# A rotation block whose end is factored into 64-wide products, with doubled squarings on TensorE and identity products written to unread PSUM

## The chip, the cores and the metric

The kernel runs on one core of a Trainium2 chip. The metric is device time in microseconds (us) of that core for one execution; of several executions the median is given. A profile is one further execution, recorded by the hardware profiler.

## The reference

Four layers run one after the other on `x` (4 batches, 512 rows, 288 channels), steered by `cond` (4, 288), all in float32. The change touches the first layer and the start of the second:

```python
U, _ = jnp.linalg.qr(P)                        # P: (288, 64)
v = silu(cond) @ W.T + b                       # 2016 numbers for each batch
A[:, iu, ju], A[:, ju, iu] = v, -v             # skew, (4, 64, 64)
R = expm(A)
z = jnp.einsum('btn,nd->btd', x, U)
z_rot = jnp.einsum('btd,bde->bte', z, R)
x = x + jnp.einsum('btd,nd->btn', z_rot - z, U)
```

Layers two to four are transformer blocks: layer norm with a shift and a scale made from `cond`, attention with 16 heads of width 18, and a feed-forward part of 1152; in the last block each row goes to two of four experts.

## The kernel before

**Layout.** `x` stays in SBUF as four tiles x0 to x3 (128 partitions, NT = 4 groups of rows, C = 288 channels). PSUM has three pools: `pmm` (one bank, 3 buffers), `pbig` (two banks, 2 buffers) and `pacc` (one bank, 1 buffer). In the rotation block and in what follows it, `pinned` is set, and every instruction of TensorE, VectorE and ScalarE goes through the helper at L60 that keeps it in the order in which it is written; so nearly all rows of the profile carry L60, and are told apart by the names of their tiles.

**The QR (L561 on).** It works on the 64x64 Gram matrix of P, one column i at a time, with two broadcasts on TensorE. `gram_step(i+1)` sends row i+1 of X to all 64 partitions (`to_all`, tile g_bc, a product of one column of the identity and the row), and VectorE makes rn, a column of Fm and the new X from it; ScalarE makes a column of Nm, GpSimd one of Rh. Then row i of Wt is broadcast in the same way (w_bc), and `sign_step` makes Hs, den, num, rec, c and the new Wt on VectorE. X, Wt and Fm of a column are needed by the next, so the columns form a chain.

**Beside the columns** run three generators, each taken a step further at fixed places of a column. `main` is `skew_and_exp`: it transposes W (p_WT), makes v (p_v), goes through DRAM to the skew matrices (p_up, then tile S, once column 33 has been reached), and then the exponential: nine products of a series (p_ser) and SQUARINGS = 16 squarings (p_sq). Since E stands for expm minus the identity, a squaring is E2 = 2E + E·E; `products` does the eight 64x64 products of the four batches on TensorE, two batches side by side in the array, and VectorE adds 2E while it evicts. `side` is `project_P` (the transposes p_t of x, and p_zP, the product of P and x) and later `first_modulations` (p_mod). `fills` clears buffers.

**The rotation's end (L582 to L598).** The 64x64 half of X that holds the elimination is transposed (p_E), copied (Em), multiplied with At, which is P transposed (p_Q), and scaled into QT (64x288). Es holds expm minus the identity of all batches with the signs Hs applied, XD the right half of X.

**`rotate(n)` (L601 to L626)** takes batches 2n and 2n+1. Each has a product Es·QT (p_RU, 64x288), a copy to RU on ScalarE, and a product with XD (p_EU); then for each of the four groups of rows one product p_xr with zP for each batch and a VectorE add into x, for both batches in turn.

**The start of attention (L1264 on).** `rotate(0)` is run to its end; then `head_biases(0)` (products p_qkb), the statistics of batch 0 (`normalize(0, 0, 0)`), and `project(0)`: transposes p_t, products p_qk and p_v, and a trip of q and k through DRAM (tiles qd). `rotate(1)` and the statistics of batch 1 are interleaved with the products of `project(0)` once q and k have been sent. Then LOOK = 10 steps of `maxima` follow (a pair of products p_s, 128x1024, and a VectorE reduce of each), each with one step of what is left of `rotate(1)`. After that the main loop over the 12 pairs of block and batch begins.

The helper behind both broadcasts of a column:

```python
def to_all(name, i, src):
    p = pbig(name)[:D, 0, :src.shape[-1]]
    matmul(p, ident[:D, i:i + 1].to_broadcast([D, D]), src, start=True, stop=True)
    return p
```

Of the kernel before, what the change touches and what calls it, by code (L numbers as in the profile page):

```python
# [9 lines left out]
F32 = mybir.dt.float32  # L10
U32 = mybir.dt.uint32
AF = mybir.ActivationFunctionType
ALU = mybir.AluOpType
# [3 lines left out]
B, T, C = 4, 512, 288  # L17
NT = 4
KC, KP = 3, 96

KW, TAIL, STRIPS = 2, 32, 3
# [12 lines left out]
D = 64  # L34
# [13 lines left out]
def cond_seq_kernel(ctx: ExitStack, tc: tile.TileContext, a: dict, out: bass.AP):  # L48
    nc = tc.nc
# [14 lines left out]
    vector, scalar = InOrder(nc.vector), InOrder(nc.scalar)  # L64
    matmul, transpose = InOrder(nc.tensor).matmul, InOrder(nc.tensor).transpose
# [7 lines left out]
    work = ctx.enter_context(tc.tile_pool(name="work", bufs=2))  # L73
    mods = ctx.enter_context(tc.tile_pool(name="mods", bufs=1))
    ps = ctx.enter_context(tc.tile_pool(name="ps", bufs=2, space=PSUM))
    blocks = ctx.enter_context(ExitStack())
    fixed = blocks.enter_context(tc.tile_pool(name="fixed", bufs=1))

    def pmm(name):
        return ps.tile([128, 512], F32, tag="mm", name=name, bufs=3)  # L80

    def pbig(name):
        return ps.tile([128, 2, 512], F32, tag="big", name=name)

    def pacc(name):
        return ps.tile([128, 512], F32, tag="acc", name=name, bufs=1)
# [11 lines left out]
    x = []  # L98
# [5 lines left out]

    ident = const.tile([128, 128], F32, name="ident")
    make_identity(nc, ident)
    ones = const.tile([1, 128], F32, name="ones")
    nc.gpsimd.memset(ones, 1.0)
    eps6 = const.tile([128, 1], F32, name="eps6")
# [92 lines left out]
    def head_biases(l):  # L202
        QB[l] = to_columns(f"qkb{l}", WA[l][3])
        if l != 1:
            vector.tensor_mul(QB[l], QB[l], scol)
# [155 lines left out]
    with tc.tile_pool(name="l0", bufs=1) as l0, tc.tile_pool(name="l0w", bufs=2) as l0w, \  # L361
            tc.tile_pool(name="scratch", bufs=1, space=bass.MemoryType.DRAM) as scratch:

        X = l0.tile([D, 2 * D], F32, name="X")
        At = l0.tile([D, C], F32, name="At")
        Wt = l0.tile([D, D], F32, name="Wt")
        pt = pmm("p_G")
        for k in range(KC):  # L370
# [5 lines left out]
            transpose(pt[:D, k * KP:(k + 1) * KP], P_in[:, k, :], ident[:KP, :KP])  # L376
        nc.vector.tensor_copy(Wt, pt[:D, :D])
        nc.scalar.copy(At, pt[:D, :C])
        minus = l0.tile([D, D], F32, name="minus")
        nc.gpsimd.memset(minus, -1.0)  # L380
        nc.gpsimd.affine_select(out=minus, in_=minus, compare_op=ALU.is_gt, fill=0.0, base=0,
# [4 lines left out]
        Hs = l0.tile([D, D], F32, name="Hs")  # L386

        def to_all(name, i, src):
            p = pbig(name)[:D, 0, :src.shape[-1]]
            matmul(p, ident[:D, i:i + 1].to_broadcast([D, D]), src, start=True, stop=True)  # L390
            return p

        def gram_step(i):
            bc = to_all(f"g_bc{i}", i, X[:, i:i + D + 1])
            rn = l0w.tile([D, 1], F32, tag="rn", name=f"rn{i}")
            vector.reciprocal(rn, bc[:, 0:1])
            vector.scalar_tensor_tensor(Fm[:, i:i + 1], X[:, i:i + 1], rn, minus[:, i:i + 1], ALU.mult, ALU.mult)
            vector.scalar_tensor_tensor(X[:, i + 1:i + D + 1], bc[:, 1:], Fm[:, i:i + 1],
                                        X[:, i + 1:i + D + 1], ALU.mult, ALU.add)
            scalar.activation(Nm[:, i:i + 1], bc[:, 0:1], AF.Sqrt, scale=0.25)  # L400
            nc.gpsimd.tensor_mul(Rh[:, i:i + 1], Fm[:, i:i + 1], Nm[:, i:i + 1])
# [15 lines left out]
        def skew_and_exp():  # L417
# [48 lines left out]
            nc.gpsimd.affine_select(out=up, in_=up, compare_op=ALU.is_gt, fill=0.0, base=0,  # L466
                                    pattern=[[0, B], [1, D]], channel_multiplier=-1)
            yield
            while column[0] < 33:
                yield  # L470
                yield
            pt = pmm("p_up")
# [11 lines left out]
            vector.tensor_scalar_mul(Sf[:, :2 * D], Sf[:, :2 * D], 0.5 ** SQUARINGS)  # L484
            yield

            def products(name, left, right):
                p = pacc(name)
                for m in range(4):
                    for h in range(2):  # L490
                        r = slice(h * D, (h + 1) * D)
                        matmul(p[r, m * D:(m + 1) * D], left[r, (m + 2) % 4, :], right[r, m, :],
                                         start=True, stop=True)
                return p[:, :4 * D]


# [5 lines left out]
                vector.scalar_tensor_tensor(E.rearrange("i m j -> i (m j)"), p, 1.0 / n, Sf, ALU.mult, ALU.add)  # L502
                yield
            for n in range(SQUARINGS):
                p = products(f"p_sq{n}", E, E)
                E2 = l0w.tile([128, 4, D], F32, tag="E", name=f"sq{n}")
                yield
                vector.scalar_tensor_tensor(E2.rearrange("i m j -> i (m j)"), E.rearrange("i m j -> i (m j)"),
                                            2.0, p, ALU.mult, ALU.add)
                yield  # L510
                E = E2

# [1 line left out]
            for b in range(B):  # L514
                scalar.copy(Eb[:, b, :], E[(b % 2) * D:(b % 2 + 1) * D, 2 + b // 2, :])
            Rm.append(Eb)


        zP = hT[1][:, 0:2, :]
        XD, Es = hT[1][0:D, KW, 0:D], hT[1][0:D, KW, D:5 * D].rearrange("p (b d) -> p b d", b=B)  # L520
        rnorm = hT[1][0:D, KW, 5 * D:5 * D + 1]
        QT = mods.tile([D, C], F32, name="QT")

        def project_P():
            for n in range(2):
# [35 lines left out]
        for i in range(D):  # L561
            column[0] = i
            if i + 1 < D:
                gram_step(i + 1)
            bc = to_all(f"w_bc{i}", i, Wt[:, i:])
            beside = i >= 6 and (i < 15 or i >= 18)
            next(main, None)
            if beside:
                next(side, None)
            sign_step(i, bc)  # L570
            next(main, None)
            if beside:
                next(side, None)
            next(fills, None)
            if i == 27:

                WA.append(load_attn(0, "L1_cond_W_qkv", "L1_cond_b_qkv", "L1_cond_W_proj", "L1_cond_b_proj"))
        for _ in main:
            pass
        for _ in side:  # L580
            pass
        preload()  # L582

        dg = l0.tile([D, 2], F32, name="dg")
        norm, sign4 = dg[:, 0:1], dg[:, 1:2]
        junk = l0.tile([D, D], F32, name="junk")
        pt = pmm("p_E")
        transpose(pt[:D, :D], X[:, D:], ident[:D, :D])
        Em = l0.tile([D, D], F32, name="Em")
        scalar.copy(Em, pt[:D, :D])  # L590
        vector.scalar_tensor_tensor(junk, Nm, 2.0, ident[:D, :D], ALU.mult, ALU.mult, accum_out=norm)
        vector.reciprocal(rnorm, norm)
        vector.scalar_tensor_tensor(junk, Hs, 4.0, ident[:D, :D], ALU.mult, ALU.mult, accum_out=sign4)
        vector.scalar_tensor_tensor(Es, Rm[0], sign4,
                                    Hs.rearrange("p (o d) -> p o d", o=1).to_broadcast([D, B, D]), ALU.mult, ALU.mult)
        pt = pmm("p_Q")
        matmul(pt[:D, :C], Em, At, start=True, stop=True)
        vector.tensor_scalar_mul(QT, pt[:D, :C], rnorm)  # L598
        scalar.copy(XD, X[:, D:])


    def rotate(n):

        ts = []
        for h in range(2):
            p = pmm(f"p_RU{2 * n + h}")
            matmul(p[:D, :C], Es[:, 2 * n + h, :], QT, start=True, stop=True)
            t = work.tile([128, C], F32, tag="gated", name=f"RU{2 * n + h}", bufs=3)
            scalar.mul(t[:D], p[:D, :C], rnorm)
            ts.append(t)  # L610
        yield 0.6
        e = work.tile([128, C], F32, tag="gate", name=f"EU{n}")
        p = pmm(f"p_EU{n}")
        for h in range(2):
            matmul(p[h * D:(h + 1) * D, :C], XD, ts[h][:D], start=True, stop=True)
        scalar.copy(e, p[:, :C])
        yield 0.6
        for j in range(NT):
            ps = pmm(f"p_xr{2 * n}_{j}"), pacc(f"p_xr{2 * n + 1}_{j}")
            for h in range(2):  # L620
                r = slice(h * D, (h + 1) * D)
                matmul(ps[h][:, :C], zP[r, n, j * 128:(j + 1) * 128], e[r], start=True, stop=True)
            for h in range(2):
                xb = x[2 * n + h][:, j, :]
                vector.tensor_add(xb, ps[h][:, :C], xb)
            yield 0.6  # L626

# [377 lines left out]
    with tc.tile_pool(name="attn", bufs=2) as at:  # L1007
# [90 lines left out]
        def maxima(G, step):  # L1098

            n, g = divmod(G, NG)  # L1100
            j, hp = divmod(step, 2)
            p = pbig(f"p_s{G}_{step}")
            for i in range(2):
                r = slice((2 * hp + i) * HS, (2 * hp + i + 1) * HS)
                matmul(p[:, i, :], Q[n % 2][r, g, j * 128:(j + 1) * 128], K[n % 2][r, g, :], start=True, stop=True)
            vector.tensor_reduce(M[G % 2][:, j, 2 * hp:2 * hp + 2, HD:HD + 1], p, AX.X, ALU.max)
# [155 lines left out]
            yield from route(b)  # L1262

        E, ready, PO, S, there, norms = [], [], [None], {}, set(), {}  # L1264
        for _ in rotate(0):
            pass
        head_biases(0)
        norm = normalize(0, 0, 0)
        for _ in norm:
            pass  # L1270
        norm1 = normalize(0, 0, 1)
        rest = rotate(1)
        sent = False
        for cost in project(0, norm):
            next(norm1, None)
            sent = sent or cost is None
            if sent and cost == 0.95:
                next(rest, None)
        norm = norm1
        for t in range(LOOK):  # L1280
            maxima(*divmod(t, 8))
            if t == 8:
                take_maxima(0)
            next(norm, None)
            next(rest, None)
# [212 lines left out]
```

## Time and profile before

| | value |
|---|---|
| three executions, us | 2103.7, 2110.49, 2111.6 |
| their median, us | 2110.49 |
| the profiled execution, us | 2122.64 |
| its span, first to last recorded work, us | 2120.9 |
| mean granted TensorE clock over the span | 0.933 |
| PE (TensorE products) busy, us | 1933.4 (91%) |
| PEld (weight loads, beside PE) busy, us | 936.0 (44%) |
| DVE (VectorE) busy, us | 933.8 (44%) |
| ACT (ScalarE) busy, us | 777.1 (37%) |
| POOL (GpSimd) busy, us | 251.3 (12%) |

The profiler's page gives these as busy time over the whole span. It also cuts the span into 40 equal slices of 53 us and writes for each engine one digit, its busy share in tenths, and in the row PEclk the granted clock in tenths of full speed. The most time by far goes to the attention and the feed-forward parts; the largest group of instructions is this one (the line of the source, engine and operation, output and inputs, shape, count, busy us and mean ns of one, then the idle time ahead of it on its engine and what ended that):

```profile
L60 DVE TENSOR_REDUCE store<-p_s 128x2 f32<-128x1024 f32 x384 | 470.2, 1225 | 385.1 <-PE p_st L60 334.0
```

The rotation block and the start of attention fill about the first 226 us. The timeline view lists single instructions there: start (us), duration (us), engine, line, operation, and output and inputs with their shapes; an entry with "x2" stands for a product or a weight load that is recorded as two.

### The profile page before, as it was taken

What the parts mean: (1) busy time and instruction counts of PE and PEld (TensorE: products, weight loads), DVE (VectorE), ACT (ScalarE), POOL (GpSimd) and SP (SyncE); (2) the same over time, 40 slices, a digit from 0 to 9 for tenths busy, and PEclk for the clock granted to TensorE, in tenths of its full rate; (3) what the DMA queues carried; (4) which work ended last, traced back from release to release, by engine and by line L of the source; (5) the groups of instructions that cost most, each with busy time, mean ns of one, the idle gap of its engine ahead of it and who ended that gap; (6) DMA issues with size and microseconds to landing.
All of it is one profiled execution on the core that took longest, in us unless ns stands there. A gap on an engine that the chain in (4) does not pass through costs nothing. (4 is left out here: it accounts for less than half of the span.)

```text
span 2120.9 us, 26102 instructions
## 1 busy us (share of the span) xinstructions
PE 1933.4 (91%) x10200; PEld 936.0 (44%) x10200; DVE 933.8 (44%) x1974; ACT 777.1 (37%) x1159; POOL 251.3 (12%) x361
## 2 busy tenths in 40 slices
PE   7778989999999999899999999998987899999997
PEld 4553322343433434334234343333322367777775
DVE  6774535526256263552643626355577134111111
ACT  5111444434345354443543434434444222112111
POOL 1000001000001020110100000000010122332322
PEclk9556899999999999989999999999999689999999
DMA  3211125122031121511213112161221355666563
GB/s 95 70 39 45 34 65 160 26 56 76 16 75 41 52 79 45 127 46 25 88 27 77 48 51 81 21 135 31 81 51 58 111 196 178 203 207 223 182 216 94
DMA packets 89418, 187.21 MB, mean 88 GB/s; under 512 B 25453, under 2 KB 50456, under 8 KB 86802
## 3 DMA queue, kind: packets, MB, share of 16 engines
q1 hardware_dynamic: 77462, 103.39, 18.8%
q0 software_dynamic: 11248, 79.79, 11.6%
q10 hardware_dynamic: 584, 2.36, 0.4%
q8 instruction: 80, 1.31, 0.3%
q14 instruction: 44, 0.36, 0.1%
HBM read 152.49 MB, written 55.45 MB: 98 GB/s over the span
## 5 line engine op out<-in xcount | busy, mean ns | idle before, releaser
L60 ACT ACTIVATE e<-p_st 128x1024 f32<-128x1024 f32 x384 | 392.7, 1023 | 692.1 <-PE p_st L60 687.8
L60 DVE TENSOR_REDUCE store<-p_s 128x2 f32<-128x1024 f32 x384 | 470.2, 1225 | 385.1 <-PE p_st L60 334.0
L60 PE MATMUL p_s<-store 32*128 32x512 f32 x1536 | 452.6, 664 | 79.7 <-DVE store L60 76.9
L60 PE MATMUL p_st<-store 32*128 32x512 f32 x1536 | 449.8, 664 | 0.9 <-DVE store L60 0.9
L60 PEld LDWEIGHTS p_s<-store 32*128 32x128 f32 x1536 | 122.7, 190 | 312.5 <-DVE store L60 221.4
L60 PE MATMUL p_av<-e,store 128*32 128x512 f32 x1536 | 213.5, 629 | 2.2 <-ACT e L60 2.2
L60 PE MATMUL p_he<-hTe,store 128*128 128x256 f32 (+1 forms) x1026 | 200.1, 404 | 4.2 <-DVE hTe L60 4.2
L60 PE MATMUL p_ye<-store,hide 128*128 128x288 f32 x684 | 175.0, 415 | 7.1 <-ACT hide L60 7.1
L60 ACT ACTIVATE hide<-p_he,store 128x256 f32<-128x256 f32 x171 | 68.5, 471 | 281.8 <-PE p_he L60 281.8
L60 PEld LDWEIGHTS p_he<-hTe,store 128*128 128x128 f32 (+1 forms) x1026 | 147.6, 191 | 53.1 <-issue 30.5
L691 POOL TENSOR_TENSOR x<-x,gated 128x288 f32<-128x288 f32 x80 | 63.4, 793 | 848.0 <-DVE gated L60 848.0
L60 PE MATMUL p_qk<-hT,wqk 128*126 128x512 f32 (+1 forms) x360 | 163.9, 626 | 0.0
L60 PE MATMUL p_h<-hT,w 128*128 128x512 f32 (+1 forms) x432 | 156.7, 618 | 5.2 <-DVE store L60 5.2
L60 PEld LDWEIGHTS p_ye<-store,hide 128*128 128x128 f32 x684 | 130.3, 193 | 46.9 <-ACT hide L60 10.9
L60 PE MATMUL p_y<-w,hid 128*128 128x288 f32 x576 | 141.8, 407 | 0.0
L60 DVE TENSOR_TENSOR gated<-p_y,gate 128x288 f32<-128x288 f32 x32 | 14.6, 457 | 285.8 <-PE p_y L60 285.8
L60 PEld LDWEIGHTS p_st<-store 32*128 32x128 f32 x1536 | 119.5, 189 | 12.4 <-issue 9.3
L60 PEld LDWEIGHTS p_y<-w,hid 128*128 128x128 f32 x576 | 108.8, 190 | 35.5 <-issue 6.1
L60 PEld LDWEIGHTS p_h<-hT,w 128*128 128x128 f32 (+1 forms) x432 | 60.7, 189 | 99.7 <-issue 83.6
L60 PE MATMUL p_o<-wp,oc 126*128 126x288 f32 (+1 forms) x288 | 101.2, 475 | 1.3 <-DVE oc L60 1.3
L60 PEld LDWEIGHTS p_qk<-hT,wqk 128*126 128x126 f32 (+1 forms) x360 | 47.8, 179 | 98.7 <-issue 98.5
L60 DVE COPY hTe<-p_te 128x512 f32<-128x512 f32 x19 | 13.1, 690 | 172.9 <-PE p_tf L60 127.8
(248 smaller groups left out, 1736.6 us busy)
## 6 DMA issues: line engine op xcount, KB each, us to landing
store<-qd SPq DMA_DIRECT2D x96, 144.0 KB
qd<-stage SPq DMA_DIRECT2D x48, 252.0 KB
od<-o SPq DMA_DIRECT2D x192, 36.0 KB
rd<-rd SPq DMA_DIRECT2D x12, 576.0 KB
oc<-od SPq DMA_DIRECT2D x24, 252.0 KB
rb<-rd SPq DMA_DIRECT2D x24, 252.0 KB
etab<-in_L_cond_w_dram SPq DMA_DIRECT2D x4, 1296.0 KB
etab<-in_L_cond_w_dram SPq DMA_DIRECT2D x8, 576.0 KB
```

The costliest lines, as they stand in the source:

```text
L60: ins = f(*args, **kw)
L691: nc.gpsimd.tensor_add(x[b][:, j, :], x[b][:, j, :], t)
```

## The change

- A new helper `keep_warm(bank, n)` issues products of the 128x128 identity with itself, n columns in all, at most 512 in one product, into a bank that nobody reads.
- One of them, of 256 columns (384 in columns 0 to 2, 29 to 32 and 52 to 63), is put into every column of the QR, after `sign_step`; its target is the second bank of the w_bc tile, which `to_all` hands out through `free`.
- `products` takes `twice`: 2E is added on TensorE, by a product of twice the identity (`two`) and E into the same PSUM tile, for both halves of the array; a squaring is then evicted by a ScalarE copy in place of VectorE's operation.
- The series may start at column 30 instead of 33, and `head_biases(0)` moves from behind `rotate(0)` into column 60.
- The rotation's end is factored in another way: Y is the right half of X with norms and signs applied, p_RY = R_b·Y and p_MT are 64x64 products for each batch, and MT·At gives what p_EU gave. p_E, p_Q, Em, QT, Es, p_RU and RU go. The diagonal of Nm is reduced in the last column.
- `rotate` does all of its first batch before its second, with two groups of rows in one `pbig` tile; of batch 0 each group is added on its own, of the others two at a time. Batch 0's statistics are interleaved with its adds.
- `keep_warm` is also put in at six places between the rotation's end and the last step of `maxima`.

```diff
+    def keep_warm(bank, n):
+
+        while n > 0:
+            w = min(n, 512)
+            matmul(bank[:, :w].rearrange("p (o m) -> p o m", m=128), ident, ident_wide[:, :w // 128, :], start=True, stop=True)
+            n -= w
...
+        two = l0.tile([128, 128], F32, name="two")
+        nc.gpsimd.tensor_scalar_mul(two, ident, 2.0)
...
         def to_all(name, i, src):
-            p = pbig(name)[:D, 0, :src.shape[-1]]
+            t = pbig(name)
+            p = t[:D, 0, :src.shape[-1]]
             matmul(p, ident[:D, i:i + 1].to_broadcast([D, D]), src, start=True, stop=True)
+            free[0] = t[:, 1]
             return p
...
-            while column[0] < 33:
+            while column[0] < 30:
...
-            def products(name, left, right):
+            def products(name, left, right, twice=False):
+
                 p = pacc(name)
+                halves = [slice(h * D, (h + 1) * D) for h in range(2)]
+                if twice:
+                    for r in halves:
+                        matmul(p[r, :4 * D], two[r, r], right[r].rearrange("i m j -> i (m j)"), start=True, stop=False)
                 for m in range(4):
-                    for h in range(2):
-                        r = slice(h * D, (h + 1) * D)
+                    for r in halves:
                         matmul(p[r, m * D:(m + 1) * D], left[r, (m + 2) % 4, :], right[r, m, :],
-                                         start=True, stop=True)
+                               start=not twice, stop=not twice or m == 3)
...
-                p = products(f"p_sq{n}", E, E)
+                p = products(f"p_sq{n}", E, E, twice=True)
...
-                vector.scalar_tensor_tensor(E2.rearrange("i m j -> i (m j)"), E.rearrange("i m j -> i (m j)"),
-                                            2.0, p, ALU.mult, ALU.add)
+                scalar.copy(E2.rearrange("i m j -> i (m j)"), p)
...
             bc = to_all(f"w_bc{i}", i, Wt[:, i:])
             beside = i >= 6 and (i < 15 or i >= 18)
+            warm = free[0]
...
+            keep_warm(warm, 384 if i < 3 or i >= 52 or 29 <= i < 33 else 256)
             next(fills, None)
...
+            if i == D - 4:
+                head_biases(0)
...
+        vector.scalar_tensor_tensor(junk, Hs, 2.0, ident[:D, :D], ALU.mult, ALU.mult, accum_out=dg[:, 2:3])
+        Y = l0.tile([D, D], F32, name="Y")
+        vector.tensor_scalar(Y, X[:, D:], dg[:, 1:2], dg[:, 2:3], ALU.mult, ALU.mult)
+        pt = pmm("p_RY")
+        for b in range(B):
+            matmul(pt[:D, b * D:(b + 1) * D], Rm[0][:, b, :], Y, start=True, stop=True)
+        warm = pbig("warm1")
+        keep_warm(warm[:, 0], 256)
+        RY = l0.tile([D, B * D], F32, name="RY")
+        vector.tensor_copy(RY, pt[:D, :B * D])
+        pt = pmm("p_MT")
+        for b in range(B):
+            matmul(pt[:D, b * D:(b + 1) * D], RY[:, b * D:(b + 1) * D], Y, start=True, stop=True)
+        keep_warm(warm[:, 0], 256)
+        vector.tensor_copy(MT, pt[:D, :B * D])
...
+            m = slice((2 * n + h) * D, (2 * n + h + 1) * D)
+            matmul(p[h * D:(h + 1) * D, :C], MT[:, m], At, start=True, stop=True)
         scalar.copy(e, p[:, :C])
         yield 0.6
...
+        for h in range(2):
+            r = slice(h * D, (h + 1) * D)
+            for i in range(0, NT, 2):
+                p = pbig(f"p_xr{2 * n + h}_{i}")
+                for j in (i, i + 1):
+                    matmul(p[:, j - i, :C], zP[r, n, j * 128:(j + 1) * 128], e[r], start=True, stop=True)
+                    if n == 0 and h == 0:
+                        xb = x[0][:, j, :]
+                        vector.tensor_add(xb, p[:, j - i, :C], xb)
+                        yield 0.3
+                if n or h:
+                    xb = x[2 * n + h][:, i:i + 2, :]
+                    vector.tensor_add(xb, p[:, :, :C], xb)
+                    yield 0.6
...
-        for _ in rotate(0):
-            pass
-        head_biases(0)
+        turn = rotate(0)
         norm = normalize(0, 0, 0)
+        next(turn)
+        keep_warm(warm[:, 0], 256)
+        for _ in range(NT):
+            next(turn)
+            next(norm)
+        keep_warm(pmm("warm2"), 3 * 512)
         for _ in norm:
             pass
+        for _ in turn:
+            pass
+        keep_warm(pmm("warm3"), 512)
...
             if sent and cost == 0.95:
                 next(rest, None)
+                keep_warm(pmm("warm4"), 512)
+        keep_warm(pmm("warm5"), 512)
         norm = norm1
         for t in range(LOOK):
             maxima(*divmod(t, 8))
+            keep_warm(pmm(f"warm6_{t}"), 256 if t > 4 else 128)
```

More of the change, by code (lines that the diff above doesn't have):

```diff
@@ L106, in cond_seq_kernel @@
     make_identity(nc, ident)
+    ident_wide = ident.rearrange("p (o m) -> p o m", o=1).to_broadcast([128, 4, 128])
     ones = const.tile([1, 128], F32, name="ones")
@@ L362, in cond_seq_kernel @@
             tc.tile_pool(name="scratch", bufs=1, space=bass.MemoryType.DRAM) as scratch:
+        zP = hT[1][:, 0:2, :]
+        MT = hT[1][0:D, KW, 0:B * D]
+        At = mods.tile([D, C], F32, name="At")
         X = l0.tile([D, 2 * D], F32, name="X")
-        At = l0.tile([D, C], F32, name="At")
         Wt = l0.tile([D, D], F32, name="Wt")
@@ L388, in to_all @@
         def to_all(name, i, src):
-            p = pbig(name)[:D, 0, :src.shape[-1]]
+            t = pbig(name)
+            p = t[:D, 0, :src.shape[-1]]
             matmul(p, ident[:D, i:i + 1].to_broadcast([D, D]), src, start=True, stop=True)
+            free[0] = t[:, 1]
             return p
+        free = [None]
         def gram_step(i):
@@ L516, in skew_and_exp @@
             Rm.append(Eb)
[L519 to L522, printed above, removed]
+            yield
         def project_P():
@@ L564, in cond_seq_kernel @@
                 gram_step(i + 1)
+            if i == D - 1:
+                dg = l0.tile([D, 3], F32, name="dg")
+                junk = l0.tile([D, D], F32, name="junk")
+                vector.scalar_tensor_tensor(junk, Nm, 2.0, ident[:D, :D], ALU.mult, ALU.mult, accum_out=dg[:, 0:1])
+                vector.reciprocal(dg[:, 1:2], dg[:, 0:1])
             bc = to_all(f"w_bc{i}", i, Wt[:, i:])
             beside = i >= 6 and (i < 15 or i >= 18)
+            warm = free[0]
             next(main, None)
@@ L582, in cond_seq_kernel @@
         preload()
[L584 to L599, printed above, removed]
-    def rotate(n):
[L604 to L611, printed above, removed]
+        vector.scalar_tensor_tensor(junk, Hs, 2.0, ident[:D, :D], ALU.mult, ALU.mult, accum_out=dg[:, 2:3])
[13 more added lines that the diff above has]
+        vector.tensor_copy(MT, pt[:D, :B * D])
+    def rotate(n):
         e = work.tile([128, C], F32, tag="gate", name=f"EU{n}")
@@ L614, in rotate @@
         for h in range(2):
-            matmul(p[h * D:(h + 1) * D, :C], XD, ts[h][:D], start=True, stop=True)
+            m = slice((2 * n + h) * D, (2 * n + h + 1) * D)
+            matmul(p[h * D:(h + 1) * D, :C], MT[:, m], At, start=True, stop=True)
         scalar.copy(e, p[:, :C])
         yield 0.6
[L618 to L626, printed above, removed]
+        for h in range(2):
[12 more added lines that the diff above has]
+                    yield 0.6
     NB, LOOK = 3 * B, 10
```

## The prediction

> **What bounds the kernel now.** I read the page's 40 slices first, because the change lies in the first 230 us of a 2120.9 us span, then windows over that stretch, then its timeline.
>
> ```profile
> PE   7778989999999999899999999998987899999997
> DVE  6774535526256263552643626355577134111111
> PEclk9556899999999999989999999999999689999999
> ...
> 10.50:80.40 69.90, 54.22 (x276) 31.66 (x275) 54.11 (x301) 30.71 (x69) 6.43 (x41) 0.76 0.33 88
> 80.40:149.00 68.60, 51.54 (x566) 40.02 (x566) 55.38 (x293) 9.95 (x45) 6.92 (x33) 0.50 0.13 31
> 149.00:173.00 24.00, 16.87 (x50) 8.90 (x51) 11.44 (x41) 4.11 (x11) 0.00 (x0) 0.50 0.00 0
> 173.00:194.80 21.80, 21.03 (x63) 8.47 (x61) 3.05 (x11) 7.89 (x14) 0.00 (x0) 0.93 0.35 99
> 194.80:226.00 31.20, 29.80 (x76) 9.42 (x77) 16.69 (x21) 0.23 (x1) 0.26 (x1) 0.53 0.03 7
> ```
>
> A window row has its length, then PE, PEld, DVE, ACT and POOL busy, then clock, DMA share and GB/s. From the second slice to the fifth TensorE has about half its clock. The 64 columns of the QR (10.5 to 149.0) keep VectorE busy for four fifths of the time. From 149 on no engine but PE is near full, and PE is slow. Each link here is on the path, since everything after 226 waits for the rotated x. One column in the timeline, with a squaring, then the same place in a later column without one, then an early one:
>
> ```profile
> 127.10 0.14 DVE L60 TENSOR_SCALAR Hs<-w_bc 64x1 f32<-64x1 f32 x1
> 127.49 0.29 PEld L60 LDWEIGHTS g_bc<-X,ident 64*64 64x64 f32 x2
> 128.10 0.22 DVE L60 SCALAR_TENSOR_TENSOR Wt<-w_bc,st,Wt 64x11 f32<-64x11 f32 x1
> 128.24 0.40 DVE L60 SCALAR_TENSOR_TENSOR sq<-sq,p_sq 128x256 f32<-128x256 f32 x1
> 128.57 0.15 DVE L60 RECIPROCAL rn<-g_bc 64x1 f32<-64x1 f32 x1
> 129.21 0.14 DVE L60 TENSOR_SCALAR Hs<-w_bc 64x1 f32<-64x1 f32 x1
> ...
> 142.93 0.21 DVE L60 SCALAR_TENSOR_TENSOR Wt<-w_bc,st,Wt 64x4 f32<-64x4 f32 x1
> 143.06 0.15 DVE L60 RECIPROCAL rn<-g_bc 64x1 f32<-64x1 f32 x1
> 143.26 0.28 PEld L60 LDWEIGHTS w_bc<-Wt,ident 64*64 64x64 f32 x2 [0.66 <-PE g_bc L60]
> ...
> 41.40 0.33 PE L60 MATMUL g_bc<-X,ident 64*64 64x65 f32 x2
> 41.76 0.16 DVE L60 RECIPROCAL rn<-g_bc 64x1 f32<-64x1 f32 x1 [0.36 <-PE g_bc L60]
> ```
>
> See that g_bc of two columns ahead was issued at 127.49, before Wt, so rn follows Wt without a pause. VectorE goes straight through: 2.11 us a column with the squaring's evict (0.33 of it, 128.24 to 128.57), 1.77 without (143.70 less 141.93), half clock or not. The 63 periods from 10.53 to 149.02 sum to 138.5 us.
>
> **The filler in the columns.** It is written after sign_step, so TensorE's order becomes: w_bc of this column, main's and side's products, filler, g_bc of two columns ahead, next w_bc. It writes the unused half of the w_bc tile, and in the built program each of the 64 fillers waits for VectorE's count at which this column's Wt update is done, the last reader of that tile. Behind it in TensorE's queue stands g_bc, and VectorE's next instruction but for the series' evict is rn, which reads g_bc. The lead of g_bc over Wt is gone. The new period, at full clock: Hs to the end of Wt 1.22 (127.10 to 128.32), VectorE to TensorE 0.12 (Wt ends 143.14, w_bc starts 143.26), filler, g_bc to rn 0.36 (41.40 to 41.76), rn to Hs 0.64 (128.57 to 129.21).
>
> The filler's price: consecutive weight loads of the 512-wide p_qk start 0.43 apart at clock 1.00 (180.34, 180.77); a product is two such issues, so 256 columns take 2 x 0.215 = 0.43 and 384 take 0.64. [...]
>
> Periods: 2.77 (256) and 2.98 (384). 45 x 2.77 + 18 x 2.98 = 178.3: **+40 us**. At half clock the filler is 0.85 or 1.28 (p_qk at 174.51 and 175.36), and g_bc to rn 0.51 (53.90 to 54.41): 3.34 and 3.77, sum 218: +80.
>
> Does 0.43 us in 2.77 hold the clock? [...] At 30 to 40, with 8 transposes a column, the clock held; in the columns of p_v, which fills 4 array columns a product, it fell at about 47. The filler is 16% of a column at full clock, with p_t, p_zP or a doubled squaring a third or more. [...] I take a third of the columns at half clock: +53.
>
> **The other edits in the columns.** The 16 squarings lose their VectorE evict; that 16 x 0.33 = 5.3 is already out of the new period, as are the series' 9 x 0.33, which now fall in the wait. The doubling adds two 64x256 products side by side, 0.43; w_bc, p_sq and doubling need about 1.2 at full clock, hidden by the 1.33 from Hs to the filler's release; without that cover (half clock) it costs about 0.4 a column. The ACT copy of 128x256 (0.3 to 0.6, nearest the 96x504 copy of 0.58) has a column to finish. Series three columns earlier: p_up's wait for up's POOL select (1.2 at 80.88) may go, but the S column still costs 1. head_biases at column 60 stands before g_bc: +2. No DMA is issued, added or moved; POOL gets one 128x128 multiply (two), at the start among its memsets. Columns in all: 53 + 3 = **+56**.
>
> **From 149 to 226**, at full clock. First add to x: 8.2 us after the last Hs now (157.17); then Y 0.5, p_RY 0.6, copy 0.4, p_MT 0.6, copy 0.4, p_EU 0.7 (193.33), copy 0.4, p_xr 0.75, seven handoffs 0.7: 5.0, saves 3.2. From there to the last statistics of batch 0: 10.7 now (eight adds, p_qkb, statistics), then 4 x (0.46 + 0.56) = 4.1: saves 6.6. The filler of 3 x 512 (2.6) with batch 1's products and 512 more stands before p_t, about 0.3 beyond VectorE: costs 0.3. The 12 p_t and first p_qk at half clock (169.8 to 176): saves 2.6. Then the p_qk stage is at full clock and the round trip of qd to 194.8 is a DMA: nothing, less 1 for three fillers. Maxima, 30 us at clock 0.53: p_s pair 1.06 (as at 232.6) against 2.08, the reduce 1.23. x's products now take the two p_s buffers, so four steps go one after the other at 2.5, six at 1.4, p_m and p_bv 1.7: 20, saves 10. Unknown ends: nothing if the clock stays low (then -13 is left of the whole), -28 if buffers don't bind. Sum **-22**.
>
> **Sum**: +56 - 22 = +34. The profiled execution took 2122.64 us (span 2120.9); the runs' median is 12 us below it. I add the 34 to both: 2157 profiled, median **2144**.
>
> **Rivals.**
> - *The clock falls, the filler doesn't do what it says* (0.20): the p_v stretch and the 0.50 in busy squaring columns speak for it, the hold at 30 to 40 against. +80 + 3, tail -18: +65, 2175.
> - *The wait is cheap* (0.15), the other side: VectorE's pause between Wt and rn is what decides. Without any wait the columns are 63 x 1.81 = 114, so net is 63w - 43 us for a pause w; it turns at w = 0.69. I have 0.96 from the rows. If g_bc's 0.36 overlaps the filler's stream and the clock is full throughout, w = 0.45 and net is -15; with a tail of -28, -21: 2090. For it: in the columns of p_WT and p_t TensorE is late anyway.
> - *The two cancel* (0.10): columns all at full clock at +40 + 3, tail -28, shifts later in the clock's dips (slice 32 has 6) of -10: about 2113.
> - The forecast 0.55.
>
> **Numbers.** Range 2105 to 2185: below it is most of the cheap wait, above it some of the fallen clock, in all under 0.2. The likeliest alone: 2125 to 2175. About 0.5% (10.5 us) can be told from no change: slower 0.76, same 0.09, faster 0.15.
>
> **What would show it.** Right: rn after Wt by about 1 us with g_bc as its releaser, g_bc right after the filler, Hs to Hs 2.7 to 3.4; last Hs past 190; p_t about 11 after it; p_s pairs at 1.06. Wrong: Hs to Hs at 1.8, or a filler that starts before Wt ends.

## The result, and the profile after

The changed kernel takes **2193.0 us** (median of 4 executions) against 2109.15 us of the kernel before beside it: ratio 1.039, 95% interval 1.035 to 1.043. It is slower, as forecast, but 2144 was forecast and the range ended at 2185. The profiled execution has a span of 2196.7 us, 75.8 more than before.

First the page of the changed kernel (40 slices, now of 55 us each):

```profile
span 2196.7 us, 26511 instructions
...
PE   7876898899999999989999999999987889999998
...
DVE  3454364562626536256262543525566334211111
...
PEclk9658699999999999999999999999999689999999
```

VectorE, which stood at 6, 7 and 7 tenths in the three slices of the columns, stands at 3, 4, 5 and 4 in the four that they take now. So the engine that set the pace waits. The windows of the same kernel show where (columns as in the prediction: length, then PE, PEld, DVE, ACT and POOL busy, clock, DMA share, GB/s):

```profile
10.70:50.00 39.30, 31.95 (x113) 19.56 (x114) 17.71 (x96) 17.88 (x29) 2.28 (x18) 1.00 0.18 58
50.00:83.00 33.00, 28.10 (x128) 13.58 (x127) 16.39 (x90) 9.24 (x24) 1.83 (x10) 0.78 0.01 3
83.00:137.00 54.00, 41.38 (x184) 21.89 (x185) 25.57 (x135) 4.63 (x18) 2.97 (x15) 0.50 0.27 67
137.00:190.00 53.00, 41.90 (x459) 28.55 (x458) 28.79 (x154) 9.92 (x39) 4.12 (x19) 0.81 0.17 39
190.00:234.50 44.50, 26.80 (x161) 15.38 (x160) 19.08 (x109) 6.03 (x24) 2.23 (x12) 0.67 0.00 1
234.50:260.00 25.50, 24.16 (x68) 12.01 (x69) 11.43 (x36) 3.38 (x7) 0.00 (x0) 0.64 0.00 1
```

The columns fill 10.7 to 234.4 and VectorE is busy less than half of it. What it waits for is one line of the view of waits (who waits for whom: us in total, times, longest), of the changed kernel over its columns:

```profile
DVE rn L60 <- PE g_bc L60: 94.4, 61, 2.2
```

The same line over the columns of the kernel before:

```profile
DVE rn L60 <- PE g_bc L60: 11.5, 20, 2.0
```

So a wait of 11.5 us in 20 times has become one of 94.4 us, in 61 of 64 columns. One column of the changed kernel at full clock, in the timeline:

```profile
64.43 0.14 DVE L60 TENSOR_SCALAR Hs<-w_bc 64x1 f32<-64x1 f32 x1
...
65.43 0.26 DVE L60 SCALAR_TENSOR_TENSOR Wt<-w_bc,st,Wt 64x48 f32<-64x48 f32 x1
65.74 0.30 PEld L60 LDWEIGHTS w_bc<-ident 128*128 128x128 f32 x2 [1.84 <-DVE Wt L60]
65.74 0.70 PE L60 MATMUL w_bc<-ident 128*128 128x256 f32 x2 [0.92 <-DVE Wt L60]
66.37 0.19 PEld L60 LDWEIGHTS g_bc<-X,ident 64*64 64x64 f32 x2 [0.33 <-issue]
66.37 0.33 PE L60 MATMUL g_bc<-X,ident 64*64 64x65 f32 x2
...
66.73 0.16 DVE L60 RECIPROCAL rn<-g_bc 64x1 f32<-64x1 f32 x1 [1.05 <-PE g_bc L60]
...
67.38 0.14 DVE L60 TENSOR_SCALAR Hs<-w_bc 64x1 f32<-64x1 f32 x1
```

This is the chain that the prediction named: Wt ends, the filler (the "w_bc<-ident" rows) starts, g_bc follows it, rn follows g_bc; VectorE stands idle for 1.05 us. The filler takes 0.63 until g_bc starts, where 0.43 was expected, and Hs to Hs is 2.95. At half clock the same link looks like this:

```profile
31.51 0.50 PEld L60 LDWEIGHTS w_bc<-ident 128*128 128x128 f32 x2 [1.22 <-DVE Wt L60]
...
32.66 0.48 PE L60 MATMUL g_bc<-X,ident 64*64 64x65 f32 x2
...
33.18 0.16 DVE L60 RECIPROCAL rn<-g_bc 64x1 f32<-64x1 f32 x1 [1.72 <-PE g_bc L60]
```

Filler to g_bc is 1.15, and the pause 1.72. The column is a half-clock one by g_bc, which takes 0.48 in place of 0.33 (0.47 in the window from 83 to 137, which has 0.50 in its clock column), though the window around it has 1.00 in its clock column; more on that at the end.

By stage, in us. "First add" and what follows count from the start of the last Hs; p_t is the transposes of project(0), p_st the first product of the main loop; the rest runs from p_st to the span's end.

| kernel | columns | first add | p_t | p_qk | p_s | p_st | rest |
|---|---|---|---|---|---|---|---|
| before | 138.5 | 8.2 | 20.8 | 23.8 | 45.8 | 74.6 | 1897 |
| changed | 223.7 | 9.8 | 22.4 | 23.9 | 46.4 | 67.9 | 1894 |

The columns (with 0.2 at their start) give +85.4, the part to p_st -6.7, the rest -2.9: together the 75.8. The rest is the same code in all kernels below, and in their profiled executions it lies between 1872 and 1898; so a difference of one span by under some 20 us is read from the stages and from the timed runs, not from the span.

### The profile page after: what moved, and what is told of

It reads as the page before. It is cut to its first block, busy times and chain, and to the rows that moved or that the text cites. A ratio compares the mean times of both kernels' runs of the same rounds, so it can differ in the third digit from the quotient of the medians.

```text
span 2196.7 us, 26511 instructions
## 1 busy us (share of the span) xinstructions
PE 1994.7 (91%) x10437; PEld 966.6 (44%) x10437; DVE 931.9 (42%) x1953; ACT 781.0 (36%) x1169; POOL 251.7 (11%) x362
## 5 line engine op out<-in xcount | busy, mean ns | idle before, releaser
L60 PE MATMUL p_s<-store 32*128 32x512 f32 x1536 | 443.5, 650 | 81.4 <-DVE store L60 79.4
L60 PE MATMUL w_bc<-ident 128*128 128x256 f32 (+1 forms) x128 | 74.9, 682 | 52.1 <-DVE Wt L60 51.8
```

Source lines behind the costliest of these rows:

```text
L60: ins = f(*args, **kw)
```

## The experiments

**The filler out of the columns.**

```diff
-            keep_warm(warm, 384 if i < 3 or i >= 52 or 29 <= i < 33 else 256)
```

> The changed kernel without the filler in the 64 columns; all fillers behind the columns stay. Theory W (the filler's wait for Wt takes the lead of g_bc away, and that alone makes the columns longer): the columns from the first Hs to the last fall from 223.7 us to about 130 (138.5 before, less 16 squaring evicts of 0.33 on VectorE and some of the starts of the series), the profiled span from 2196.7 to about 2103. Rival D (the doubling on TensorE with a ScalarE evict, the earlier series or the moved head biases hold the columns up): the columns stay above 150.

Columns 136.5, span 2090.5, ratio 0.995 (0.993 to 0.998). One line carries the loss of the columns, 87 us; the other edits together leave the columns 2 us shorter than before. That they stop at 136.5 and not at 130 is taken up with the squarings.

**The filler alone.** The kernel before with `keep_warm`, `free` and the one line above, nothing else.

> The kernel before with nothing but the column filler of the change, at its place and with its widths. Theory W: the columns take 220 to 230 us as in the changed kernel (138.5 before), and the span is 2120.9 + 85 = about 2206, a little more than the changed kernel, which gains some 10 us behind the columns. Rival D: well under that, since the other edits are missing.

Columns 227.9, span 2200.5, ratio 1.042 (1.036 to 1.047). The filler by itself makes the slowdown, and the rest of the change takes back about 4 us of columns.

**The wait without the work.**

```diff
-            keep_warm(warm, 384 if i < 3 or i >= 52 or 29 <= i < 33 else 256)
+            matmul(warm[:, 0:1], ident, ident[:, 0:1], start=True, stop=True)
```

> The column filler reduced to a product of one column, at the same place with the same wait for Wt. Theory W: the wait, a weight load and g_bc behind it remain, so Hs to Hs is about 2.5 at full clock and 2.8 at half, columns 160 to 175, span about 2140. Rival P: with the work gone the columns fall to those of the kernel without the filler.

Columns 197.6, ratio 1.025 (1.020 to 1.031). A product of a single column still costs 61 us over no product, so it is not the streaming alone that the columns cannot hold. The expected 160 to 175 us was 22 us or more too small. The timeline of this kernel:

```profile
120.28 0.24 DVE L60 SCALAR_TENSOR_TENSOR Wt<-w_bc,st,Wt 64x28 f32<-64x28 f32 x1
...
120.57 0.50 PEld L60 LDWEIGHTS w_bc<-ident 128*128 128x128 f32 x2 [1.09 <-DVE Wt L60]
120.58 0.59 PE L60 MATMUL w_bc<-ident 128*128 128x1 f32 x2 [0.91 <-DVE Wt L60]
...
121.09 0.47 PE L60 MATMUL g_bc<-X,ident 64*64 64x65 f32 x2
...
121.61 0.16 DVE L60 RECIPROCAL rn<-g_bc 64x1 f32<-64x1 f32 x1 [0.75 <-PE g_bc L60]
```

The filler's 128-wide weights are loaded twice, and that stands behind Wt: 0.52 us from 120.57 to 121.09 for one column. That is the term that the price "2 x 0.215" left out; with 256 columns only part of it is added, since the filler then takes 1.15 where 0.85 was expected at half clock. And g_bc is at 0.47 from the start to 150 us, so most columns have the half-clock period, 2.94 to 3.00.

**The same filler, not behind Wt.** At the same place in TensorE's order, with the second bank of g_bc's tile as target in place of w_bc's:

```diff
+            warm = free[0]
             bc = to_all(f"w_bc{i}", i, Wt[:, i:])
             beside = i >= 6 and (i < 15 or i >= 18)
-            warm = free[0]
```

> The changed kernel with one line moved: the column filler stays at its place in TensorE's order and keeps its widths, but writes the second bank of g_bc's tile, whose last readers on VectorE and ScalarE (X and Nm) are done early in the column, in place of w_bc's, whose last reader is Wt. Theory W: without the wait for Wt the columns fall from 223.7 us to between 125 and 165, for at the same place the filler starts before Wt ends and g_bc is early again where TensorE has room. Rival P (TensorE's work in the column, not the wait): they stay above 190.

Columns 171.1, ratio 1.015 (1.009 to 1.020): 52.6 us less than the changed kernel for a moved line. At the same clock a column with 256 takes 2.15 in place of 2.93 us, or 2.82 in place of 3.62, so this is not a better clock alone. The wait for Wt is thus most of the 87 us. The columns are 6 us over the expected range, and 34.6 us remain over the kernel without filler. The timeline of this kernel shows where they arise:

```profile
147.13 0.70 PE L60 MATMUL g_bc<-ident 128*128 128x256 f32 x2
...
147.74 0.22 DVE L60 SCALAR_TENSOR_TENSOR Wt<-w_bc,st,Wt 64x13 f32<-64x13 f32 x1
147.88 0.19 PEld L60 LDWEIGHTS g_bc<-X,ident 64*64 64x64 f32 x2 [0.46 <-PE g_bc L60]
```

The filler now starts at 147.13, 0.6 before Wt, but the next g_bc writes the same tile, waits for the filler's end (0.46 without work on TensorE) and comes only just as Wt ends. Hs to Hs is 2.15 at full clock, and 2.8 to 3.3 in the columns at half clock, where the filler takes 1.15 or more.

**The filler directly behind g_bc**, between g_bc and its first reader:

```diff
             bc = to_all(f"g_bc{i}", i, X[:, i:i + D + 1])
+            if i > 0:
+                n = i - 1
+                keep_warm(free[0], 384 if n < 3 or n >= 52 or 29 <= n < 33 else 256)
```

> The same fillers, of the same widths, but each directly behind g_bc in the second bank of g_bc's tile, so that none waits for Wt. Theory W: at full clock the filler (0.43) ends before Wt does, and Hs to Hs is about 1.8; at half clock (0.85) w_bc is late by about 0.4 and it is 2.3; columns between 115 and 150, span between 2090 and 2125. Rival P (it is TensorE's work itself, not the wait, that the columns cannot hold): Hs to Hs stays over 2.8 and the columns above 180.

Columns 160.1, span 2121.3, ratio 1.010 (1.007 to 1.013). The span is in the range, the columns are 10 us over it: the shortest take 2.02 to 2.13 at full clock, not 1.8, since w_bc waits for the filler's end here:

```profile
72.80 0.30 PEld L60 LDWEIGHTS g_bc<-ident 128*128 128x128 f32 x2
73.53 0.19 PEld L60 LDWEIGHTS w_bc<-Wt,ident 64*64 64x64 f32 x2 [0.43 <-PE g_bc L60]
```

This is the cheapest of the three places tried, and TensorE is at full clock (g_bc 0.33) from 40 to 159 us except for a dip from 84 to 95; yet the columns are 23.6 us longer than with no filler and TensorE mostly at half clock. Without a filler, VectorE waits for g_bc 13.4 us in all 136.5, so a faster TensorE has not much more than that to give there. A filler that stands in the way of neither broadcast, in a tile of its own, was not tried.

**A wider filler at the place of the change**: `keep_warm(warm, 1024)`.

> The changed kernel with 1024 columns in each column filler, at the same place. If TensorE's share of work in a column is what holds its clock, then g_bc takes 0.33 throughout and Hs to Hs is 2.95 + 768 columns by 0.43/256 = 4.2: columns about 265. If it doesn't, g_bc takes 0.47 and Hs to Hs is 3.62 + 768 by 0.85/256 = 6.2: columns about 390.

One execution: columns 290.6, span 2251.4. Hs to Hs is 4.2 in most columns and g_bc 0.33, as computed for full clock; in the first three, five in the middle and the last seven it is mostly 5 to 6.2, and g_bc goes back to 0.47 there, hence 290.6 and not 265. 768 columns more cost 4.24 - 2.95 = 1.29 us, or 0.43 for 256: the streaming price of the prediction was right, it was the weight loads that were missing from it. And with four times the work the columns stay at the full-clock period far longer, 106 us at a time. In the changed kernel g_bc went from 0.33 to 0.47 between 66.4 and 69.8 us, with 256 columns in 2.95 us beside p_v, though with 256 and 384 in 2.92 and 3.12 it stayed at 0.33 for 48 us beside the doubled squarings.

**The squarings back on VectorE**, in the kernel without the column filler: `products` without `twice`, and VectorE's 2E + p as before.

> The kernel without the column filler, with the squarings as before: no doubling on TensorE, VectorE adds 2E while it evicts. If the doubling's gain is the 16 x 0.33 us taken from VectorE, the columns rise from 136.5 to about 141. Rival: the wait for the ScalarE copy and the longer product group have taken that gain back, and the columns stay at 135 to 138.

Columns 138.7, ratio 0.999 (0.996 to 1.003). The doubling is worth 2.2 us of columns in these two profiles, not 5.3; that lies between the two readings (about 141, or 135 to 138). In the kernel without the column filler its new round trip, and what the clock makes of it, can be seen in the timeline:

```profile
105.94 0.28 DVE L60 SCALAR_TENSOR_TENSOR X<-g_bc,Fm,X 64x64 f32<-64x64 f32 x1
...
106.37 0.77 ACT L60 COPY md<-p_mod 4x288 f32<-4x288 f32 x2
...
107.57 0.37 ACT L60 COPY sq<-p_sq 128x256 f32<-128x256 f32 x1
...
108.00 0.65 PE L60 MATMUL p_sq<-sq,two 64*64 64x256 f32 x4 [0.23 <-ACT sq L60]
...
121.29 1.12 PE L60 MATMUL p_sq<-sq,two 64*64 64x256 f32 x4 [0.18 <-ACT sq L60]
122.20 1.06 PE L60 MATMUL p_sq<-sq 64*64 64x64 f32 x16
...
123.51 0.16 DVE L60 RECIPROCAL rn<-g_bc 64x1 f32<-64x1 f32 x1 [0.64 <-PE g_bc L60]
...
126.11 0.65 PE L60 MATMUL p_sq<-sq,two 64*64 64x256 f32 x4 [0.34 <-ACT sq L60]
126.59 0.63 PE L60 MATMUL p_sq<-sq 64*64 64x64 f32 x16
...
127.52 0.15 DVE L60 RECIPROCAL rn<-g_bc 64x1 f32<-64x1 f32 x1
```

At 106 to 108 ScalarE does other copies first, and the next squaring, which stands before g_bc in TensorE's order, waits for its copy. At 121 to 124, at half clock, the longer squaring makes rn wait 0.64, and Hs to Hs is 2.50 where the same columns with the squaring on VectorE take 2.11; at 126 to 128, at full clock, there is no wait and it is 1.77. So VectorE's 0.33 a squaring is gone, but a part of it comes back as a wait for g_bc (13.4 us over these columns, 10.6 with the squarings on VectorE), and most of that where the clock is low. Here a faster TensorE does help.

**No filler at all**, and **fillers only from p_qk on** (the three of 256 columns in the rotation's end, the 1536 and the 512 before p_t taken out; both without the column filler):

> The changed kernel without any filler. Against the kernel without the column filler (columns 136.5 us; from the last Hs the first p_t 22.1 and the first p_st 67.6 us later). Theory S (the fillers between the rotation's end and p_t stand in front of products that are due, at half clock 0.5 each for the first three and about 4 for the 1536 columns): p_t comes 16 to 18 us after the last Hs. What the later fillers are worth shows in p_st: at 70 or later if they hold the clock of p_qk and the maxima, at 63 or earlier if those are at full clock anyhow. Rival: p_t stays at about 22, the fillers lie in gaps.

> No filler in the columns and none before p_t; those among the products p_qk, before the maxima and in the maxima stay. Theory S: p_t 16 to 18 us after the last Hs as without any filler, and p_st some 5 us sooner than the 67.6 of the kernel without the column filler, so about 63; span about 2086, the shortest of all. Rival: with TensorE at half clock in p_t and p_qk the gain is given back (67 or later).

| kernel | columns | first add | p_t | p_qk | p_s | p_st | rest |
|---|---|---|---|---|---|---|---|
| without the column filler | 136.5 | 8.9 | 22.1 | 23.6 | 46.1 | 67.6 | 1876 |
| no filler at all | 137.0 | 7.1 | 15.1 | 18.0 | 39.4 | 69.2 | 1898 |
| fillers from p_qk on | 136.4 | 7.1 | 15.1 | 18.0 | 40.8 | 62.3 | 1897 |

Ratios 0.9965 (0.993 to 1.000) without any, 0.992 (0.989 to 0.995) with those from p_qk on. The fillers before p_t cost 7.0 us. In the kernel without the column filler it reads so in the timeline:

```profile
149.00 1.22 PE L60 MATMUL warm<-ident 128*128 128x256 f32 x2
149.11 0.42 DVE L60 COPY RY<-p_RY 64x256 f32<-64x256 f32 x1 [1.20 <-PE p_RY L60]
150.15 0.93 PEld L60 LDWEIGHTS p_MT<-Y,RY 64*64 64x64 f32 x8 [0.65 <-DVE RY L60]
...
160.71 5.49 PE L60 MATMUL warm<-ident 128*128 128x512 f32 x6
...
163.38 1.45 DVE L60 TENSOR_SCALAR xn<-x,mv,rstd 128x288 f32<-128x288 f32 x4
...
166.12 1.77 PEld L60 LDWEIGHTS p_xr<-EU,hT 64*128 64x128 f32 x8 [1.50 <-issue]
```

RY is there at 149.53: the gap that the filler was to fill, from 149.00, is 0.5 us. At half clock the filler takes 1.15, so p_MT comes 0.6 late, at 150.15. It happens three times. The 1536 columns run to 166.1, and the first xn lay ready at about 163.8. The fillers from p_qk on do what they are for: p_s to p_st is 21.5 us with them, 29.8 without. These are the windows of that stretch, with them and then without any:

```profile
187.80:209.20 21.40, 21.40 (x83) 9.06 (x82) 15.13 (x14) 0.00 (x0) 0.00 (x0) 1.00 0.00 1
187.00:216.80 29.80, 29.10 (x66) 10.36 (x66) 15.13 (x15) 0.00 (x0) 0.00 (x0) 0.53 0.05 10
```

The stages met the expectation or came a little earlier (p_t 15.1 against 16 to 18, p_st 62.3 against 63), the span did not (2106 for 2086): its rest is 1897 where the other kernel's is 1876, for the same code. By the timed runs this version has the lowest ratio, 0.8% (0.5 to 1.1%) under the kernel before, and 4.5% under the changed one (0.992 against 1.039); its interval overlaps that of the kernel without the column filler (0.993 to 0.998), so these two cannot be told apart.

**Both together**: those fewer fillers, and the column filler at its place but not behind Wt.

> The same, with the fillers before p_t taken out as in the kernel that keeps only those from p_qk on. If the unread products in the columns bring TensorE to p_t at full clock, p_t and p_qk come 1 to 3 us sooner after the last Hs than the 18.0 of that kernel (p_qk), and the first p_st at about 60; whether the whole beats it depends on the columns, which have to stay under 139.

Columns 171.0, p_t 15.7, p_qk 18.6, p_st 63.5, ratio 1.012 (1.006 to 1.017). p_qk was expected at 15 to 17, p_st at 60, the columns under 139: nothing is gained for the 34.7 us of columns, since the clock falls in the last of them (g_bc 0.47), before the tail begins.

## Why the prediction was wrong in size

The mechanism was right: the filler waits for Wt, g_bc stands behind it, rn behind g_bc, and 61 columns pause. Moving that wait away took 52.6 us off, and the rival on the fast side, the cheap wait, has fallen: its pause had to be under 0.69 us, and it was 1.05 or 1.72.

The sum was +34 and is +75.8; of the 42 us, 29.4 are in the columns, 15.3 in the tail, less 2.9 in the rest.

- **"I take a third of the columns at half clock: +53" is the step that failed most.** The third was an estimate between +40 and +80, and no run shows it. By Hs to Hs, 43 of the 63 columns are at half clock (the first 12, then 24, then the last 7). With the prediction's own periods this share in place of one third is about 14 us more. The evidence lay in the profile before: g_bc takes 0.47 or 0.48 there until 28 us (the line below), 0.33 from 29 to 46, and 0.42 to 0.48 after that. I had read the clock from the windows' column, and only from 30 on.

```profile
21.41 0.47 PE L60 MATMUL g_bc<-X,ident 64*64 64x65 f32 x2
```

- **The filler's price.** 0.63 and 1.15 us for 256 columns, not 0.43 and 0.85: the loading of the weights behind the wait. The full-clock periods became 2.93 and 3.12 (2.77 and 2.98 expected), the half-clock ones 3.62 and 4.03 (3.34 and 3.77): 0.16 on 20 columns and about 0.27 on 43 are 15 us. The row chosen for it, back-to-back p_qk, has its weight loads hidden beside the product before: 0.19 of PEld in each 0.43, beside 9.42 us of unbroken PE from 172.80 on. The wider filler shows the row's 0.43 for 256 further columns of f32 (1.29 for 768).
- **The clock.** The rival in which it falls (2175) was the nearer one. With the filler of one column TensorE is busy for 59.94 of the 80 us from 60 to 140, and that did not bring the full clock: g_bc takes 0.47 there. Nor did the filler of the change do its own work in the columns: in the profiled executions TensorE has its full clock for 61 of their 224 us with it, and for 48 of 136.5 without it.
- **The other edits in the columns: +3.** About right: over the periods above the columns hold some 3 us more, and column 60 with the head biases takes 6.03 us in the changed kernel where its neighbours take 4.00, the 2 that was expected.
- **The tail: -22, measured -6.7.** "Costs 0.3 beyond VectorE" for the fillers before p_t was the wrong term: 7.0 without the column filler. The first add, -3.2 in the sum, comes at +1.7 with the fillers and -1.0 without, because p_RY, p_MT and p_EU are at half clock, 1.1 to 1.2 each against my 0.6 to 0.7. Batch 0's statistics gain without them: p_t comes 5.7 earlier than before. p_t and p_qk save 1.5 of the 2.6. The trip of q and k to p_s is about the same (22.5 against 22.0), as said. The maxima save 7.3 of the 10.
- **Slips in the working.** The terms of the tail add up to -21, not -22: the 1 us for three fillers was left out. In the cheap-wait rival, 0.96 less 0.36 is a pause of 0.60 and a net of -5, not 0.45 and -15. And the clock's row reads 5, 5, 6 and 8 in slices two to five, so the fifth is not at about half. None of these changes the outcome.

## What to carry to other kernels

Work that nobody reads is not free where it stands ahead of work that is due, here 87 us of columns: look up what its target makes it wait for (here a write into an unused bank of a tile waited for Wt, the last reader of the bank beside it, and g_bc for a filler in the second bank of its own tile, 0.46 us of idle PEld), and ask what is queued behind it. Ask first what a faster engine can win at most: here VectorE sets the pace of most columns and waits 13.4 us for g_bc in all of them, and the cheapest filler tried cost 23.6. Put a filler where the wait is long and outside the core's own chain (here the trip of q and k and the maxima: 21.5 us from p_s to p_st with fillers, 29.8 without), and make it shorter than its gap at the slow clock, not at the fast one (here 1.15 us at half clock in a gap of 0.5).

## What the runs showed of the hardware

The clock column read 1.00 here while products took as long as in stretches where it reads 0.50. In the windows of the kernel with the filler of one column:

```profile
60.00:140.00 80.00, 59.94 (x410) 43.64 (x411) 46.64 (x247) 11.24 (x39) 5.17 (x27) 1.00 0.19 47
```

g_bc takes 0.47 us in that stretch (121.09 above), as in stretches marked 0.50. The same holds in the kernels before and after the change. In the changed kernel the trace's records of the clock begin only at 55.0 us, between a g_bc of 0.47 (54.42) and one of 0.32 (57.52), and the column shows 1.00 ahead of them; it changes for the first time at 68.7, when the clock falls. In the kernel before they begin at 29.2, after a g_bc of 0.47 (27.00) and ahead of one of 0.33 (29.34). Ahead of these records the column was no measurement, and the duration of a repeated product (g_bc, 0.47 or 0.33) was the better probe.

What holds the clock is not settled by these runs: with 256 columns in each 2.02 to 2.15 us, g_bc stayed at 0.33 for 40 us and more, and with 1024 in 4.2 us too; with 256 in 2.95 us beside p_v it went to 0.47. The same code does not always do the same: the two kernels with the filler not behind Wt have the same columns, and the full clock (g_bc 0.33) that began at 31 us lasted to 79 in one and to 59 in the other.
